# Attention in a four-layer kernel: block transposes of Q and K without duplicated columns, centred weights, norms from sums of squares, other virtual times, more PSUM banks

## The chip, the cores and the metric

One NeuronCore of a Trainium2 chip runs the whole program. The metric is the device time of one execution in microseconds (us); lower is better. The time before is 798.83 us, the median of three runs (794.63 to 799.25). A profile is one further execution: that of before took 792.66 us, of which the profile's span is 790.9 us.

Engines are named as in the profile: PE multiplies matrices, PEld loads its weights, DVE and ACT work on vectors, POOL is the small general engine, and SP issues DMAs. Each engine takes its instructions strictly in program order (weight loads may run ahead of multiplications). A multiplication of f32 data stands in the profile as two records.

## The reference

The input x has 16 sequences of 256 tokens with 256 channels. Four blocks follow, each inside a residual sum and a layer norm without weights:

```
x = _layernorm(x + _L0_attn_ref(x, ...))   # Fourier mixing, 16 heads
x = _layernorm(x + _L0_ffn_ref(x, ...))    # gated low-rank experts
x = _layernorm(x + _L1_attn_ref(x, ...))   # softmax attention
x = _layernorm(x + _L1_ffn_ref(x, ...))    # ternary weights, 1024 hidden
```

The first block multiplies x by two matrices, takes a Fourier transform over each head's 16 channels, normalises, takes a running sum of the second over the tokens, multiplies and transforms back. The second chooses one of eight experts per token by a gate (its score is divided by the squared distance of the token from an expert's centre) and adds the expert's rank-8 update; it scales x by one minus the gate. The third is attention with 16 heads of 16 channels:

```
qkv = jnp.einsum('bld,ed->ble', x, W_qkv)
qkv = qkv.reshape(b, 3, H, L, D_H)
Q, K, V = (qkv[:, 0], qkv[:, 1], qkv[:, 2])
scores = jnp.einsum('bhqd,bhkd->bhqk', Q, K) * D_H ** (-0.5)
attn = jax.nn.softmax(scores, axis=-1)
out = jnp.einsum('bhqk,bhkd->bhqd', attn, V)
out = out.transpose(0, 2, 1, 3).reshape(b, L, D_IN)
return jnp.einsum('bld,ed->ble', out, W_o)
```

The reshape is a plain one: the 256 x 768 numbers of one sequence, read in memory order, are cut into 48 pieces (16 heads each of Q, K, V) of 256 rows by 16. So token l gives the rows 48 l to 48 l + 47 of that list, and "row q of head h" is not token q.

The fourth block multiplies by ternary weights, squares a ReLU, normalises and multiplies back.

## The kernel before

**Stages.** The 16 sequences go in four groups of four (`GB`). Per sequence there is a front (`front`: blocks 1 and 2, up to the transposed result x2T) and a back (`back`: block 4); per group there is one `attention`. While the attention of group i runs, the fronts of group i + 1 and the backs of group i - 1 fill the gaps. Before the first attention stand loads, folded weights, the four fronts of group 0 and eight blocks of ternary weights; after the last stand four backs.

**Who sets the order.** All work is recorded as operations with a priority and an estimated cost on one or two engines. A list scheduler (`Order.run`) then walks through virtual time, gives each operation its engine and its buffer, and writes the instructions in that order. The order on each engine is therefore fixed before the program runs. An operation's priority (`order.prio`) is its virtual time: for group i, base = 100 (i + 1); projections of the attention (QKV) stand at base - 60, scores for the maximum at base + 6 (n - 8) for the n-th head, scores for the exponential and the product with V at base + 6 n, fronts of the next group at base + 23 + 20 g, backs of the group before at base + 20 + 20 g. `order.limit` bounds how many of the eight PSUM banks fronts and backs ("r", 4) and attention ("a", 6) may hold.

**Attention.** QKV is computed 32 tokens of all four sequences at a time (a token block, `tb`, L831): 512 and 256 columns. For the six token blocks that hold Q and K, DVE turns 32 x 32 blocks from PSUM into the tile `zt` (L840), in which sequence g owns partitions 32 g to 32 g + 31 and the 16 channels of a head lie on the first 16 of them. A head's piece is 16 columns wide, but a block is 32: so each 16-column piece is read twice (`to_broadcast([P, nj, 2, HD])`), and the second copy is not used. `zt` needs a 17th row per head: ones for K (`rowk`, L858) and minus the row maximum for Q (`rowq`, L914), both put there by DMAs of one partition each. V goes to DRAM (`vd`, L849) and comes back with its rows on partitions (`v`, L868).

For each head PE computes scores (L894, four sequences side by side, 16 rows each), DVE takes the negated maximum (`nm`, L903, four per head). After four heads the maxima are transposed (L907), copied (L908, `nmT`) and sent to the 17th row (8 DMAs if the heads' numbers are not consecutive, else 4). Then PE computes the scores again with 17 rows and the other way round (L933), ACT takes the exponential (L942), and PE multiplies by V (L948). The result is turned (L956), divided (L957, L960), transposed (L977), multiplied by `wo1` (L991) and added to x2 (L999).

**Norms.** `layernorm` takes mean and variance with two `bn_stats` (L569) and two `bn_aggr` (L571) on DVE, the power -1/2 on POOL (L563, L564), two more POOL steps for the bias (L573, L574), and the scaling of each half on DVE (L577) or ACT (L582), whichever the scheduler picks. It stands four times per sequence: after blocks 1, 2, 3 and 4. In a front ACT also squares x1 with a running sum (L723) for the distance in the gate.

**SP.** One queue issues all DMAs of the program. Its order, too, is the scheduler's, which counts 0.43 us per issue (`ISSUE`) and at least 1.6 us more to the landing.

Of the kernel before, what the change touches and what calls it, by code (L numbers as in the profile page):

```python
# [14 lines left out]
ALU = mybir.AluOpType  # L15
# [270 lines left out]
def forward(ctx, tc, x, xt, wq, wkv, wo0T, f0, degen, cs, wqkvT, wo1T, wfc, wproj, cst, out):  # L286
# [23 lines left out]
    ztv = zt_.rearrange("p (l j) -> p j l", j=NJ)  # L310
# [29 lines left out]
    order.limit = {("ps", "r"): 4, ("ps", "a"): 6, ("lane", "r"): 4}  # L340
# [155 lines left out]

    def ternary(n, w_dram, store):
# [68 lines left out]
    def layernorm(y, dst, extra=()):  # L566
# [8 lines left out]
        for t in range(2):  # L575
# [10 lines left out]
            op([(DVE, 0.36, on_dve), (ACT, 0.36, on_act)], [(dst, t)], [y, mv, rs, nb, *extra])  # L586
# [3 lines left out]
    def front(b, early):  # L590
# [123 lines left out]
        layernorm(y, x1, extra)  # L714
# [4 lines left out]
        x1sq, sq1 = stat(2), w(P, 2, D)  # L719
        for t in range(2):  # L720
            act(
                [(x1sq, t), (sq1, t)], [x1, *extra], 256 + 220,
                lambda t=t: A.activation(sq1.v[:, t, :], x1.v[:, t, :], AF.Square, accum_out=x1sq.v[:, t : t + 1]),  # L723
            )
# [80 lines left out]
        layernorm(y2, x2, extra)  # L805
# [13 lines left out]
    def attention(i):  # L819
# [4 lines left out]
        for n, tb in enumerate((5, 2, 0, 3, 6, 7, 1, 4)):  # L824
            order.prio = base - 60.0 + n
            for j0, nj in ((0, 32), (32, 16)):
# [10 lines left out]
                if tb < ZT:  # L837
                    dve(
                        [(z[tb], j0)], [b], nj * 32,
                        lambda b=b, tb=tb, j0=j0, nj=nj: V.transpose(  # L840
                            ztv[:, j0 : j0 + nj, ts(tb, 32)], b.v.unsqueeze(2).to_broadcast([P, nj, 2, HD])
                        ),
                        us=nj * 32 * 1.72e-3,
                    )
                if tb >= VT // 32:
# [7 lines left out]
                    )  # L853

            heads = [h for h in range(H) if k_at(h) == tb]
            for g in range(GB if heads else 0):
                op(
                    (SP, 0.1, lambda g=g, lo=ZQ + heads[0] * S, n=len(heads) * 2: nc.sync.dma_start(  # L858
                        zt_[32 * g + HD : 32 * g + HD + 1, lo : lo + n * P].rearrange("o (c q) -> o c q", q=P),
                        a(ones)[0:1, :].unsqueeze(1).to_broadcast([1, n, P]),  # L860
                    )),
                    [(rowk[tb], g)], [ones, z[tb]],
                )
        order.prio = base - 20.0
        for half, lo, n, at in ((0, 28, 4, 12), (0, 0, 12, 0), (1, 12, 16, 0)):
            for g in range(GB):
                op(
                    (SP, 0.5, lambda g=g, half=half, lo=lo, n=n, at=at: nc.sync.dma_start(  # L868
                        va[half][:, at : at + n, g, 0:HD],
                        vd.slot.ap[g].rearrange("t e -> (t e)")[(2 * ZQ + lo * P) * HD - VT * NJ * HD :][: n * P * HD].rearrange("(n p d) -> p n d", p=P, d=HD),  # L870
                    )),
                    [(v[half], (g, at))], [vd],
                )

        def part(g, rows, which, h, at=0, n=S):
            lo = which * ZQ + h * S + at
            return zt_[32 * g : 32 * g + rows, lo : lo + n]
# [7 lines left out]
        for q in range(4):  # L885
            nm, nmT, heads = tile_("nm", [P, GB, 4, 2]), tile_("nmT", [32, P]), HEADS[4 * q : 4 * q + 4]
            for k, h in enumerate(heads):
                order.prio = base + 6.0 * (4 * q + k - 8)
                sc = [ps([P, 2, S], "a") for _ in range(GB)]

                def go(sc=sc, h=h):
                    for t in range(2):
                        for g in range(GB):
                            T.matmul(  # L894
                                sc[g].v[:, t, :], part(g, HD, 0, h, t * P, P), part(g, HD, 1, h),
# [4 lines left out]
                for g in range(GB):  # L900
                    dve(
                        [(nm, (k, g))], [sc[g]], 512,
                        lambda nm=nm, sc=sc, g=g, k=k: V.tensor_reduce(nm.v[:, g, k, :], sc[g].v, AX.X, ALU.max, negate=True),  # L903
# [3 lines left out]
            pe([b], [nm, small], 0.11, lambda b=b, nm=nm: T.transpose(b.v, nm.v.rearrange("p g h t -> p (g h t)"), ident))  # L907
            act([nmT], [b], 128, lambda b=b, nmT=nmT: A.copy(nmT.v, b.v))  # L908
            runs = [heads] if heads[3] - heads[0] == 3 else [heads[0:2], heads[2:4]]
            for g in range(GB):  # L910
                for r, run in enumerate(runs):
                    n = len(run) * 2
                    op(
# [240 lines left out]
```

## Time and profile before

| what | value | where it is from |
|---|---|---|
| median of three runs | 798.83 us (794.63 to 799.25) | times |
| profiled execution, its span | 792.66 us, 790.9 us | times, page |
| granted TensorE clock, mean | 0.921 | times |
| instructions | 15,263 | page |
| QKV begins (L831), groups 0 to 3 | 100.1, 238.4, 421.5, 589.9 us | trace |
| first scores for the exponential (L933), groups 0 to 3 | 152.6, 291.4, 477.2, 642.4 us | trace |
| end of the last group's output projection (L991) | about 723 us | trace |

Busy time is the union of an engine's instructions. A PE that is "busy" may be at half clock, or a record may be stretched by a wait, so busy time is not work. In the view of windows each row gives a stretch, its length, and the busy time of each engine with the number of instructions, then the granted clock, the DMA share and GB/s. In the rows of instruction groups stand the line, engine, operation, tiles, shapes and number, then busy us, mean ns of one, and the idle time of the engine before them.

### The profile page before, as it was taken

To read this page: it belongs to the slowest core of one execution; us is meant where nothing else is said; L and a number is where in the kernel's file an instruction comes from. 1 tells how busy PE (TensorE), PEld (TensorE's weight loads), DVE (VectorE), ACT (ScalarE), POOL (GpSimd) and SP (SyncE) were. 2 spreads that over 40 slices of the span, in tenths; PEclk is the share of its full clock that TensorE was granted. 3 is DMA by queue.
4 is the path that set the end of the run, shared out by engine and by line. 5 is a ranking of instruction groups with operands and counts; after the bars stand their busy time and mean duration, and the time that the engine had idled before them with its cause. 6 is when DMAs were issued, how large, how long until landed. Compare 5 with 4: busy or idle time off the path is not lost.

```text
span 790.9 us, 15263 instructions
## 1 busy us (share of the span) xinstructions
PE 744.1 (94%) x5664; PEld 527.2 (67%) x5664; DVE 642.3 (81%) x1513; ACT 476.6 (60%) x942; POOL 124.0 (16%) x306
## 2 busy tenths in 40 slices
PE   9999499999999999999999999999989999999794
PEld 6786256665566667777676767765566787766784
DVE  1999989888987997998789999897567978756554
ACT  5865531238782238988765644966721297875973
POOL 1022000101110020222122012021020002011123
PEclk9999699679999988999999989997989699999986
DMA  8101015200001450001011350000001700000000
GB/s 292 40 27 41 13 24 79 57 15 16 29 15 25 67 69 2 16 27 30 2 40 49 60 38 16 15 16 2 15 1 35 76 10 16 14 16 15 1 28 27
DMA packets 87662, 27.18 MB, mean 34 GB/s; under 512 B 68700, under 2 KB 84900, under 8 KB 87588
## 3 DMA queue, kind: packets, MB, share of 16 engines
q1 hardware_dynamic: 87588, 26.21, 15.7%
q8 instruction: 45, 0.74, 0.4%
q14 instruction: 29, 0.24, 0.1%
HBM read 16.76 MB, written 8.91 MB: 32 GB/s over the span
## 4 chain that ended last, share of the span: by engine, by line
PE 68%; DVE 18%; ACT 9%; issue 3%; POOL 2%; DVEq 0%; ACTq 0%; POOLq 0%
PE bank L831 10%; PE bank L894 9%; PE bank L948 8%; PE bank L933 8%; PE bank L1056 7%; PE bank L609 5%; DVE nm L903 5%; PE bank L1027 5%; PE bank L991 3%; PE bank L708 3%; PE bank L793 2%; PE bank L732 2%; DVE st L569 2%; ACT zt L942 1%; ACT hi L1044 1%
## 5 line engine op out<-in xcount | busy, mean ns | idle before, releaser
L942 ACT ACTIVATE zt<-bank 128x512 f32<-128x512 f32 x256 | 133.4, 596 | 57.2 <-PE bank L933 52.3
L903 DVE TENSOR_REDUCE nm<-bank 128x2 f32<-128x512 f32 x256 | 158.8, 679 | 11.1 <-PE bank L894 10.2
L563 POOL TENSOR_SCALAR st<-st 128x2 f32<-128x2 f32 x80 | 23.4, 293 | 535.6 <-DVE st L571 369.7
L894 PE MATMUL bank<-zt 16*128 16x256 f32 x1024 | 100.4, 445 | 2.2 <-DVE nm L903 1.7
L894 PEld LDWEIGHTS bank<-zt 16*128 16x128 f32 x1024 | 63.7, 205 | 29.9 <-DVE nm L903 8.7
L831 PE MATMUL bank<-wqr,x2T 128*128 128x512 f32 (+1 forms) x256 | 83.2, 486 | 0.0
L933 PE MATMUL bank<-zt 17*128 17x256 f32 x1024 | 82.5, 415 | 0.3 <-DVE nm L903 0.3
L948 PE MATMUL bank<-zt,v 128*32 128x256 f32 x1024 | 78.6, 412 | 0.0
L1027 PE MATMUL bank<-xs,w1T 128*128 128x256 f32 x512 | 75.3, 299 | 0.5 <-DVE xs L1017 0.4
L1056 PE MATMUL bank<-w2T,hi 128*128 128x256 f32 x256 | 72.1, 312 | 3.5 <-ACT hi L1044 2.5
L1056 PE MATMUL bank<-w2T,lo 128*128 128x256 f32 x256 | 69.1, 302 | 6.0 <-DVE lo L1046 6.0
L1027 PEld LDWEIGHTS bank<-xs,w1T 128*128 128x128 f32 x512 | 67.6, 199 | 9.2 <-issue 3.7
L840 DVE STREAM_TRANSPOSE zt<-bank 128x1024 f32<-128x1024 f32 (+1 forms) x48 | 64.2, 1456 | 11.3 <-PE bank L831 5.0
L831 PEld LDWEIGHTS bank<-wqr,x2T 128*128 128x128 f32 x256 | 48.5, 190 | 34.2 <-issue 28.5
L933 PEld LDWEIGHTS bank<-zt 17*128 17x128 f32 x1024 | 51.8, 191 | 22.5 <-issue 12.4
L609 PE MATMUL bank<-wf,x 128*128 128x512 f32 x128 | 62.8, 623 | 0.0
L1056 PEld LDWEIGHTS bank<-w2T,hi 128*128 128x128 f32 x256 | 52.8, 206 | 14.1 <-issue 9.1
L564 POOL TENSOR_TENSOR st<-st,mhalf 128x2 f32<-128x2 f32 x80 | 59.4, 743 | 6.8 <-POOL st L563 0.2
L1056 PEld LDWEIGHTS bank<-w2T,lo 128*128 128x128 f32 x256 | 52.7, 206 | 7.5 <-DVE lo L1046 7.5
L1046 DVE TENSOR_TENSOR lo<-work,hi 128x512 fp32r<-128x512 f32 x64 | 42.7, 681 | 15.9 <-ACT hi L1044 15.8
L948 PEld LDWEIGHTS bank<-zt,v 128*32 128x32 f32 x1024 | 29.7, 114 | 35.1 <-issue 14.8
L1036 ACT ACTIVATE work<-bank 128x512 f32<-128x512 f32 x64 | 37.8, 591 | 20.4 <-PE bank L1027 16.2
(196 smaller groups left out, 1260.2 us busy)
## 6 DMA issues: line engine op xcount, KB each, us to landing
x<-in_xT SPq DMA_DIRECT2D x16, 256.0 KB
out<-work SPq DMA_DIRECT2D x16, 256.0 KB
x<-in_x SPq DMA_DIRECT2D x12, 256.0 KB
vd<-work SPq DMA_DIRECT2D x12, 256.0 KB
v<-vd SPq DMA_DIRECT2D x16, 128.0 KB
vd<-work SPq DMA_DIRECT2D x12, 128.0 KB
v<-vd SPq DMA_DIRECT2D x16, 96.0 KB
oT<-in_wfc SPq DMA_DIRECT2D x4, 256.0 KB
```

The costliest lines, as they stand in the source:

```text
L564: pool([dst], [dst, mhalf], 0.7, lambda: G.tensor_tensor(dst.v, dst.v, a(mhalf)[:, 0:n], ALU.pow))
L609: T.matmul(pb.v.rearrange("p a s k -> p (a s k)"), xT.v[:, c, ts(t, P)], a(wf)[:, c].rearrange("p a s f -> p (a s f)"), start=(c == 0), st ...
L831: T.matmul(b.v.rearrange("p j d -> p (j d)"), x2T.v[:, c, tb].rearrange("p g k -> p (g k)"), a(wqr)[:, c, j0 * HD : (j0 + nj) * HD], start ...
L840: lambda b=b, tb=tb, j0=j0, nj=nj: V.transpose(ztv[:, j0 : j0 + nj, ts(tb, 32)], b.v.unsqueeze(2).to_broadcast([P, nj, 2, HD])),
L894: T.matmul(sc[g].v[:, t, :], part(g, HD, 0, h, t * P, P), part(g, HD, 1, h), start=True, stop=True,)
L903: lambda nm=nm, sc=sc, g=g, k=k: V.tensor_reduce(nm.v[:, g, k, :], sc[g].v, AX.X, ALU.max, negate=True),
L933: T.matmul(sc[g].v[:, c, :], part(g, HD + 1, 1, h, c * P, P), part(g, HD + 1, 0, h), start=True, stop=True,)
L942: act([e], [sc[g]], 512, lambda e=e, sc=sc, g=g: A.activation(e.v, sc[g].v, AF.Exp, scale=HD ** -0.5))
L948: T.matmul(av.v[32 * g : 32 * g + 32, hk, :], v_part(g, h, c), es[g].v[:, c, :], start=(c == 0), stop=(c == 1),)
L1027: T.matmul(pb.v[:, i, :], a(w1T)[:, n // 2, ts(q * 2 + i, P)], xs.v[:, n % 2, n // 2, :], start=(n == 0), stop=(n == 3),)
L1046: dve([(lo, q)], [h, (hi, q)], 512, lambda h=h, part=part: V.tensor_tensor(part(lo), h.v, part(hi).bitcast(F32), ALU.subtract), us=0.63)
L1056: T.matmul(pw.v[:, t, :], part.v[:, k, ts(t, P)], a(w2T)[:, k, :], start=(k + n == 0), stop=(k + n == HID // P),)
```

## The change

Five things change together.

1. **Transposes without duplicates.** A block of 32 columns now holds two neighbouring heads' pieces, so one pass over 512 (or 256) columns turns all. The even pieces land on partitions 0 to 15 of each sequence's 32, the odd ones on 16 to 31. Four DMAs per token block (48 KB each, one per sequence) move the odd ones to partitions 0 to 15 of the second half of the 48 x 192 columns. Each head's rows now lie in two halves (even and odd), so the ones, the maxima and V's rows are written by twice as many DMAs, each half as long; the matrix products read the moving operand in two pieces of 128 columns.
2. **Centred weights.** `dg` (experts) and `wo1` get their mean over the output channels subtracted once, at the start. The sums before the second and third norm then have mean zero, because x1 and x2 have it already.
3. **Norms from sums of squares.** For those two norms ACT squares with a running sum instead of `bn_stats` and `bn_aggr` on DVE; the two POOL steps for the bias fall away. The squared length of x1 comes from its variance on POOL (three steps) instead of two squarings on ACT.
4. **Virtual times.** QKV moves from base - 60 to base, maxima from base - 48 + 6 n to base - 30 + 6 n, exponentials from base + 6 n to base + 10 + 6 n, fronts from base + 23 + 20 g to base + 20 g, backs from base + 20 + 20 g to base + 45 + 10 g. The estimate for scaling on ACT in `layernorm` goes from 0.36 to 0.53 us.
5. **PSUM banks.** The limits go from 4 to 5 (fronts and backs) and from 6 to 7 (attention).

```diff
+    ODD = ZT * 32 * NJ // 2
+    ztv = zt_[:, 0:ODD].rearrange("p (l j) -> p j l", j=NJ // 2)
+    zt2 = zt_[:, 0 : 2 * ODD].rearrange("p (t c) -> p t c", t=2)
...
-    order.limit = {("ps", "r"): 4, ("ps", "a"): 6, ("lane", "r"): 4}
+    order.limit = {("ps", "r"): 5, ("ps", "a"): 7, ("lane", "r"): 4}
...
+    def centred():
+
+        for t, at, n in ((dg, lambda: a(dg), 72), (wo1, lambda: a(wo1)[:, 0], P), (wo1, lambda: a(wo1)[:, 1], P)):
+            junk, m = tile_("work", [P, D]), stat(1)
+            act(
+                [junk, m], [t], 476,
+                lambda at=at, n=n, junk=junk, m=m: A.activation(
+                    junk.v[0:n, :], at(), AF.Identity, scale=-1.0 / D, accum_out=m.v[0:n, :]
+                ),
+            )
+            act(
+                [t], [t, m], 256,
+                lambda at=at, n=n, m=m: A.activation(at(), at(), AF.Identity, bias=m.v[0:n, :]),
...
+    def layernorm_of_centred(y, dst, extra=()):
+
+        vs, rs = stat(2), stat(2)
+        for t in range(2):
+            act(
+                [(vs, t), (dst, t)], [y, *extra], 256 + 220,
...
+                lambda t=t: A.activation(dst.v[:, t, :], y.v[:, t, :], AF.Square, accum_out=vs.v[:, t : t + 1]),
+            )
+        rsqrt(rs, lambda: vs.v, vs, 1.0 / D, LN_EPS, 2)
...
+            op([(DVE, 0.36, on_dve), (ACT, 0.36, on_act)], [(dst, t)], [y, rs, *extra])
...
+        mv, rs = layernorm(y, x1, extra)
...
-        x1sq, sq1 = stat(2), w(P, 2, D)
-        for t in range(2):
-            act(
-                [(x1sq, t), (sq1, t)], [x1, *extra], 256 + 220,
-                lambda t=t: A.activation(sq1.v[:, t, :], x1.v[:, t, :], AF.Square, accum_out=x1sq.v[:, t : t + 1]),
-            )
+
+        x1sq = stat(2)
+        pool([x1sq], [mv], 0.27, lambda: G.tensor_scalar(x1sq.v, mv.v[:, :, 1], float(D), None, ALU.mult))
+        for _ in range(2):
+            pool([x1sq], [x1sq, rs], 0.25, lambda: G.tensor_tensor(x1sq.v, x1sq.v, rs.v, ALU.mult))
...
-        layernorm(y2, x2, extra)
+        layernorm_of_centred(y2, x2, extra)
...
-            order.prio = base - 60.0 + n
+            order.prio = base + 0.0 + n
...
-                            ztv[:, j0 : j0 + nj, ts(tb, 32)], b.v.unsqueeze(2).to_broadcast([P, nj, 2, HD])
+                            ztv[:, j0 // 2 : (j0 + nj) // 2, ts(tb, 32)],
+                            b.v.rearrange("p (j t) d -> p j (t d)", t=2),
                         ),
-                        us=nj * 32 * 1.72e-3,
+                        us=nj * HD * 1.43e-3,
...
+            if tb < ZT:
+                width = 32 * NJ // 2
+                for g in range(GB):
+                    op(
+                        (SP, 0.1, lambda g=g, lo=tb * width: nc.sync.dma_start(
+                            zt_[32 * g : 32 * g + HD, ODD + lo : ODD + lo + width],
+                            zt_[32 * g + HD : 32 * g + 2 * HD, lo : lo + width],
+                        )),
+                        [(z[tb], ("odd", g))], [(z[tb], 0), (z[tb], 32)],
+                    )
...
-                order.prio = base + 6.0 * (4 * q + k - 8)
+                order.prio = base + -30.0 + 6.0 * (4 * q + k)
...
-                                sc[g].v[:, t, :], part(g, HD, 0, h, t * P, P), part(g, HD, 1, h),
+                                sc[g].v[:, t, :].rearrange("p (t q) -> p t q", t=2), some(g, HD, 0, h, t), every(g, HD, 1, h),
...
-                order.prio = base + 6.0 * n
+                order.prio = base + 10.0 + 6.0 * n
...
-            layernorm(y, x3)
+            layernorm_of_centred(y, x3)
...
-            base = 100.0 * (i + 1) + 20.0 + 20.0 * g
+            base = 100.0 * (i + 1)
             if i > 0:
-                order.prio = base
+                order.prio = base + 45.0 + 10.0 * g
                 back((i - 1) * GB + g, False)
             if i + 1 < NG:
-                order.prio = base + 3.0
+                order.prio = base + 0.0 + 20.0 * g
```

In the built order of the changed kernel SP issues 600 DMAs instead of 296 (192 for maxima instead of 96, 128 rows of ones instead of 64, 96 V loads instead of 48, and 96 moves of odd pieces). DVE scales 72 halves of norms instead of 50, and ACT 56 instead of 78.

## The prediction

> **What bounds the kernel now.** First the busy line and the slices: which engine could be the limit, and where.
>
> ```profile
> PE 744.1 (94%) x5664; PEld 527.2 (67%) x5664; DVE 642.3 (81%) x1513; ACT 476.6 (60%) x942; POOL 124.0 (16%) x306
> DVE  1999989888987997998789999897567978756554
> PEclk9999699679999988999999989997989699999986
> ```
>
> PE seems full, but it is busy also at half clock and while stretched by waits. So I counted PE's real work: every record by the shortest steady start-to-start time of its form in this trace (429 ns for 512 columns, 216 for 256, 109 for 128, 117 for the reduced-precision 256 columns of the back, 72 for the side-by-side ones, 16 of which take 1.15 us in the chain). The sum is 656.6 us. The span is 790.9 us, so 134 us are not filled: 21 before 100 us, 29 in the tail after 722 us, and 84 in the four groups. Windows show what stands in those places.
>
> ```profile
> 100.00:153.00 53.00, 52.57 (x285) 35.60 (x283) 47.32 (x76) 12.84 (x26) 1.71 (x5) 0.87 0.34 54
> 238.00:291.00 53.00, 53.00 (x313) 33.28 (x311) 47.52 (x84) 12.24 (x27) 3.33 (x11) 1.00 0.38 60
> 421.00:477.00 56.00, 54.76 (x346) 37.52 (x344) 52.33 (x92) 31.68 (x61) 5.98 (x11) 0.94 0.37 50
> 540.00:590.00 50.00, 44.68 (x374) 29.03 (x371) 29.02 (x91) 26.72 (x57) 8.13 (x24) 0.80 0.02 7
> 590.00:642.00 52.00, 51.64 (x289) 36.06 (x288) 44.28 (x65) 16.74 (x33) 3.75 (x11) 0.84 0.35 45
> 722.00:791.00 69.00, 51.63 (x327) 47.29 (x325) 38.71 (x92) 44.02 (x79) 18.34 (x40) 0.84 0.05 16
> ```
>
> Third number: PE, fifth: DVE, sixth: ACT. The first three and the fifth row are the openings of the groups, from QKV to the first exponential scores: 52 to 56 us each, with DVE 85 to 93% busy and ACT idle. Transposes (16.0 us per group by the same view for line L840) and maxima (19.8 to 22.3 us) are most of it. PE's counted work there is 43.4, 50.0, 48.0 and 40.6 us. The fourth row is the end of group 2, where no engine is full: QKV of group 3 waits for the last fronts. PE's work is 35.4 us of 50.
>
> Last, SP, since the first scores with 17 rows need its DMAs.
>
> ```profile
> SPq L868 <- DMA vd<-work: 33.7, 4, 8.4
> 144.71 5.03 SPq L914 DMA_DIRECT2D zt<-nmT  x8
> ```
>
> Each group waits about 8 us for V to land in DRAM before it is read back. Eight small issues take 5.03 us, 0.62 us each in steady pitch. In group 0 they end at 149.7 and L933 starts at 152.6, released by DVE: SP is just in time. In group 1 they end at 288.1 and L933 starts at 291.4, so 3.3 us to landing and start.
>
> **Transposes.**
>
> ```profile
> L840 DVE STREAM_TRANSPOSE zt<-bank 128x1024 f32<-128x1024 f32 x24 | 45.3, 1890 | 9.9 <-PE bank L831 5.0 <-DMA zt<-ones 2.9 <-ACT work L369 2.0
> L840 DVE STREAM_TRANSPOSE zt<-bank 128x512 f32<-128x512 f32 x24 | 24.5, 1022 | 1.4 <-ACT work L369 1.4
> L956 DVE STREAM_TRANSPOSE work<-bank 128x512 f32<-128x512 f32 x32 | 22.8, 712 | 24.6 <-PE bank L948 24.4
> L569 DVE BATCH_NORM_STATS2 st<-work 128x6 f32<-128x256 f32 x116 | 43.8, 415 | 0.7
> L571 DVE BATCH_NORM_AGGREGATE st<-st 128x2 f32<-128x6 f32 x128 | 18.6, 171 | 0.0
> L723 ACT ACTIVATE work<-work 128x256 f32<-128x256 f32 x28 | 11.4, 411 | 0.8 <-DMA vd<-work 0.8
> L723 ACT ACTIVATION_READ_ACCUMULATOR work<-work 128x1 f32 x28 | 5.5, 195 | 0.0
> L582 ACT ACTIVATE x<-work,st,st 128x256 f32<-128x256 f32 x35 | 20.0, 597 | 33.0 <-POOL st L574 32.8
> ```
>
> After there are 24 of 512 and 24 of 256 columns. By L956 (1.39 ns a column) that is 25.6 us, by the short L840 (2.00) 36.8. L956 writes contiguously, L840 with a stride as the new one does: I take 31. From 69.8 us this saves 39 (33 to 44) of DVE, some 8 us of each opening (busy union).
>
> **Norms.** 64 bn_stats and 64 bn_aggr go: 64 x 0.586 = 37.5 us of DVE. ACT gains 64 squares at 0.411 + 0.195 = 38.8 and loses 32, 19.4. The scheduler moves scalings: 22 more on DVE at 0.405 (L577), +8.9; ACT 59 fewer at 0.597 and 37 new ones with a scale alone, between 0.411 and 0.597, say 0.5: -16.7. Eight more evacuations on DVE at 0.686, +5.5, and 8 fewer on ACT, -4.7. Two squares of the back go to ACT, 1.3 each way. Centring is 6 ACT steps once, 3.3 us, in the first 50 us beside half-idle ACT; uncovered it costs 3.3. Sums: DVE -39 - 37.5 + 8.9 + 5.5 - 1.3 = -63, ACT about +3, POOL -17.1 + about 13. POOL's three steps for x1 lie beside the transposes and products of x1; if not, 0.8 us per front, 16 fronts. Strided `oT` copies and moving operands in two pieces I cost at nothing: two of 128 columns (218 ns) equal one of 256 (216). Bounds: if stride doubled a copy, 0.59 x 16 = 9 us on ACT, mostly covered.
>
> **SP.** 304 more issues at 0.62 are 188 us of SP. From the first V write to the end of the first maxima, group 0 has 44 issues before and 87 after. After: 87 x 0.62 = 54 us, plus three waits of about 2 us, each for a landed move before the ones may be written (bounds 0 and 3.3), plus 7 for V, plus 3.3 to the start: some 70 us from QKV's start instead of 52.5. With QKV at 96, L933 starts at 166, not 152.6. In groups 1 to 3 the new order lets QKV start beside the last heads of the group before and puts maxima ahead of V: 60, 47 and 47 issues to their end, 45 us with waits in group 1, against 47 us of PE work that stands before L933 there. But then L948 (product with V) waits for V: writes, 8 us, eight loads, landing. Counting what stands between, PE stalls in groups 1 to 3 about 16, 18 and 10 us, and behind a stalled L948 wait all later scores and the backs.
>
> The Trainium skill, page "DMA: Bandwidth & Descriptors", section "Rules for kernel authors", speaks against this part: transfers under 64 KB pay mostly overhead and should be made into one. With that page's fixed cost of about 2 us for each, strictly one after another, an estimate would be 608 us more. The trace overlaps them: 0.62 us of issue each.
>
> **The sum**, on the span of 790.9. Before group 0, DVE is 94% busy (74.85 of the 80 us from 20 on) and loses four norms of 1.17 us: -4. Group 0: L933 13 later, then 85 us with 74.5 of DVE shrink by 8: +5. Groups 1 to 3, opening to middle: counted gaps of 48 us before (3.0 + 10.5, 8.0 + 6.6, 11.4 + 8.5) against 44 of SP stalls: -4. End of group 2: fronts have earlier virtual times, QKV fills 10 of the 14.6 idle us: -10. Tail: one norm shorter, -1. Together -14: span 777, run 778.7 with the 1.8 around it. The run before (792.66) lies 0.8% under its median, so 785. PSUM limits and virtual times have no price of their own; they are in the order I counted.
>
> **Rivals.** *SP decides (slower).* If landings take 2 us more at the three or four waits of a group (4 x 4 x 2 = 32 us), or PE falls to half clock after each stall (before: 13.65 us long at 137 and 290 us, 7 lost each, 28 in all), some 30 come on top: 809, by the median 815. It decides once the first maxima land later than about 50 us after QKV starts; in group 0 they do. Against it: groups 1 to 3 start QKV earlier. *DVE's relief reaches PE (faster).* If SP keeps ahead, each opening shrinks by 6 us, 24 in all, with -4, -12 and -1: 752, by the median 758. For it: DVE is 85 to 93% busy in openings. Against: SP's count. *Nothing moves.* PE's order keeps as many gaps as before; DVE merely idles: 797.
>
> The Trainium skill, "TensorE: Matmul & The Clock Gate", Part 1, says an idle window of about 3.4 us halves the clock; rows here agree (0.80 in the idle end of group 2). It adds only to the first rival.
>
> **How the numbers follow.** Forecast 785 (own range 774 to 797): 45%. SP decides, 800 to 830: 25%. DVE's relief, 748 to 770: 18%. Nothing moves: 12%. The range 758 to 818 leaves out half of each outer case. Within 1% (791 to 807) a measurement of this kernel tells nothing from no change. Faster by more: 34 of the forecast's 45, the 18 and 2 of the last: 54. Slower: the 25, and 2 of each of the two middle cases: 29. Same: 17.
>
> **What would show it.** Right: DVE near 580 us; L840 near 31 us in all; L933 of group 0 at about 166 us with a gap released by the maxima's DMA; L831 no longer one block of 20.6 us; end of group 2 filled. Wrong: SP idle long before L933 (then the gain is larger), or L948 waiting over 20 us for V in several groups and a clock below 0.9 (then slower).

## The result and the profile after

The changed kernel takes 840.1 us (median of four runs, 838.45 to 842.61) against 798.81 us for the kernel before in the same comparison: ratio 1.0532, 95% interval 1.0486 to 1.0577. It is slower. Medians are of all runs, while ratios compare only runs in the faster of two states in which a kernel is found from one execution to the next, so a ratio need not be that of the medians. The profiled execution took 842.61 us, with a span of 840.8 us and a mean granted clock of 0.902 (before 0.921).

The page of the changed kernel: the busy line, and the slices of DVE and of the granted clock.

```profile
PE 762.3 (91%) x5664; PEld 531.1 (63%) x5664; DVE 609.2 (72%) x1413; ACT 477.3 (57%) x987; POOL 120.4 (14%) x290
DVE  2999869659977873979879584999567557952564
PEclk9999689779999995989999896999899688997986
```

DVE did lose work, 33 us of it, and PE is "busy" for 18 us longer with the same 5664 matrix instructions. By the shortest steady times the matrix work is the same in both kernels (654.6 us counted again for both), so the part of the span that PE does not fill went from some 136 to some 186 us. The clock row has fewer nines, 25 instead of 29: added up from the trace's record of the clock, PE stood at half clock for 168 us instead of 127.

The view of waits of the changed kernel, PE's rows that name a DMA (total us, number of times, longest us). Before, no row of PE in this view named a DMA.

```profile
PE bank L949 <- DMA zt<-zt: 22.9, 5, 7.8
PE bank L988 <- DMA zt<-nmT: 12.0, 6, 6.4
PE bank L1003 <- DMA v<-vd: 1.2, 3, 0.4
```

L949 are the scores for the maxima (L894 before) and wait for the moves of the odd pieces. L988 are the scores with 17 rows (L933 before) and wait for the maxima. L1003 is the product with V (L948 before); it hardly waits, so the stall that the prediction looked for there stands elsewhere. Where, the windows show: an opening and the stretch behind it for groups 0 and 1, then the end of group 2 and the stretch behind the opening of group 3, with the columns explained above.

```profile
98.00:153.00 55.00, 50.47 (x269) 31.59 (x267) 44.14 (x89) 13.18 (x29) 3.15 (x10) 0.93 0.26 50
153.00:174.00 21.00, 10.88 (x61) 5.25 (x53) 7.36 (x18) 4.41 (x10) 2.69 (x7) 0.58 0.41 47
245.00:298.00 53.00, 51.36 (x364) 30.70 (x357) 42.41 (x82) 19.93 (x51) 3.92 (x9) 0.97 0.16 32
298.00:342.00 44.00, 34.98 (x263) 24.42 (x267) 24.62 (x61) 18.29 (x37) 5.57 (x15) 0.81 0.39 55
580.00:620.00 40.00, 37.73 (x337) 22.37 (x338) 23.90 (x59) 21.24 (x49) 7.63 (x16) 0.87 0.09 22
652.00:700.00 48.00, 40.10 (x291) 32.22 (x293) 26.76 (x51) 27.52 (x50) 2.18 (x4) 0.72 0.38 48
```

The openings (first and third row) are nearly full. Behind the openings no engine is full: in the second row PE is busy for half of the time, at a clock of 0.58, and DVE for a third; in the fourth and sixth row the clock is 0.81 and 0.72. These two stretches and that in the second row follow the first maxima of their groups. What stands there in group 0 is in SP's timeline (start, us, instruction, number)

```profile
144.22 13.77 SPq L918 DMA_DIRECT2D v<-vd  x24
158.08 9.71 SPq L969 DMA_DIRECT2D zt<-nmT  x16
167.89 5.96 SPq L896 DMA_DIRECT2D zt<-zt  x8
```

and in PE's (the brackets: idle us before, and what ended it).

```profile
160.95 1.19 PE L988 MATMUL bank<-zt 17*128 17x256 f32 x2 [6.43 <-DMA zt<-nmT]
162.91 1.19 PE L988 MATMUL bank<-zt 17*128 17x256 f32 x2 [0.77 <-DMA zt<-nmT]
165.32 1.19 PE L988 MATMUL bank<-zt 17*128 17x256 f32 x2 [1.23 <-DMA zt<-nmT]
167.74 2.04 PE L988 MATMUL bank<-zt 17*128 17x256 f32 x10 [1.23 <-DMA zt<-nmT]
```

The maxima themselves had been ready for 20 us, as ACT's timeline shows.

```profile
138.10 0.24 ACT L963 COPY nmT<-bank 32x128 f32<-32x128 f32 x1
```

SP issues 24 loads of V before the first maxima, then 16 small DMAs of maxima at 0.61 us each. PE takes one sequence of a head after another as they land, two records of a head's 16 at a time. The whole head is done at 169.8; before, the first scores with 17 rows began at 152.6. In group 1 it is a move that PE waits for. SP's timeline first, then PE's:

```profile
303.30 15.35 SPq L918 DMA_DIRECT2D v<-vd  x24
318.75 2.78 SPq L896 DMA_DIRECT2D zt<-zt  x4
```

```profile
321.83 3.41 PE L949 MATMUL bank<-zt 16*128 16x256 f32 x16 [7.84 <-DMA zt<-zt]
```

DVE had turned token block 4 by 298.6 us, but its four moves stand behind 24 loads of V on SP, and PE stands for 7.8 us. The same gap is in groups 2 and 3, with 5.0 and 6.2 us; there 4 and 5 DMAs of ones stand between the loads and the moves as well. In the trace's record of the clock, half clock begins 1.9 to 2.9 us after PE stops in each of these four long stands (6.43, 7.84, 4.99 and 6.17 us) and lasts for 13.7 to 20.5 us. By group, the time that PE does not fill is:

| us not filled by PE | before | after | difference |
|---|---|---|---|
| up to group 0 | 23.2 | 21.8 | -1.4 |
| group 0 | 21.7 | 33.4 | +11.7 |
| group 1 | 13.2 | 28.9 | +15.7 |
| group 2 | 29.3 | 35.6 | +6.3 |
| group 3 | 20.0 | 37.7 | +17.7 |
| tail | 28.8 | 28.9 | +0.1 |

The tail is counted from the start of the last group's last output projections (722.5 us before); they end at 729.7, not at about 723.

Last, the groups of instructions after, where the change saved work: the two shapes of the transposes, and the new squares on ACT.

```profile
L877 DVE STREAM_TRANSPOSE zt<-bank 128x512 f32<-128x512 f32 x24 | 34.8, 1449 | 17.6 <-PE bank L867 16.9 <-issue 0.4 <-PE bank L1003 0.4
L877 DVE STREAM_TRANSPOSE zt<-bank 128x256 f32<-128x256 f32 x24 | 19.8, 823 | 4.7 <-PE bank L867 4.3 <-ACT work L372 0.4
L613 ACT ACTIVATE x<-work 128x256 f32<-128x256 f32 x60 | 24.5, 413 | 30.5 <-DVE work L1054 24.4 <-DVE work L836 5.9
```

The transposes cost 54.6 us, not 31: half the columns, but 2.83 and 3.2 ns a column where there were 1.85 and 2.00.

### The profile page after: what moved, and what is told of

It reads as the page before. It is cut to its first block, busy times and chain, and to the rows that moved or that the text cites. A ratio compares the mean times of both kernels' runs of the same rounds, so it can differ in the third digit from the quotient of the medians.

```text
span 840.8 us, 15583 instructions
## 1 busy us (share of the span) xinstructions
PE 762.3 (91%) x5664; PEld 531.1 (63%) x5664; DVE 609.2 (72%) x1413; ACT 477.3 (57%) x987; POOL 120.4 (14%) x290
## 4 chain that ended last, share of the span: by engine, by line
PE 63%; DVE 13%; SPq 8%; DMA 6%; ACT 5%; issue 3%; POOL 1%; DVEq 0%; ACTq 0%; POOLq 0%
PE bank L949 9%; PE bank L1003 8%; PE bank L988 8%; PE bank L1111 7%; PE bank L867 6%; PE bank L1082 6%; SPq L918 5%; PE bank L646 4%; DMA vd<-work 4%; PE bank L1046 3%; DVE zt L877 2%; PE bank L745 2%; PE bank L573 2%; SPq L969 2%; PE bank L768 1%
## 5 line engine op out<-in xcount | busy, mean ns | idle before, releaser
L949 PE MATMUL bank<-zt 16*128 16x256 f32 x1024 | 98.0, 436 | 23.0 <-DMA zt<-zt 22.9
L988 PE MATMUL bank<-zt 17*128 17x256 f32 x1024 | 93.0, 436 | 13.6 <-DMA zt<-nmT 12.0
L949 PEld LDWEIGHTS bank<-zt 16*128 16x128 f32 x1024 | 61.1, 200 | 56.2 <-issue 23.7
L867 PE MATMUL bank<-wqr,x2T 128*128 128x512 f32 (+1 forms) x256 | 94.8, 514 | 1.6 <-DVE zt L877 1.4
L988 PEld LDWEIGHTS bank<-zt 17*128 17x128 f32 x1024 | 56.9, 200 | 44.0 <-issue 20.5
L1003 PE MATMUL bank<-zt,v 128*32 128x256 f32 x1024 | 80.6, 423 | 1.5 <-DMA v<-vd 1.2
L1111 PE MATMUL bank<-w2T,lo 128*128 128x256 f32 x256 | 72.0, 309 | 7.4 <-DVE lo L1101 7.4
L1111 PE MATMUL bank<-w2T,hi 128*128 128x256 f32 x256 | 75.0, 320 | 3.5 <-ACT hi L1099 2.8
L1082 PEld LDWEIGHTS bank<-xs,w1T 128*128 128x128 f32 x512 | 70.5, 210 | 7.8 <-issue 3.5
L877 DVE STREAM_TRANSPOSE zt<-bank 128x512 f32<-128x512 f32 (+1 forms) x48 | 52.4, 1136 | 22.3 <-PE bank L867 21.2
L1091 ACT ACTIVATE work<-bank 128x512 f32<-128x512 f32 x64 | 37.7, 589 | 33.9 <-PE bank L1082 33.8
L1003 PEld LDWEIGHTS bank<-zt,v 128*32 128x32 f32 x1024 | 29.7, 116 | 42.8 <-issue 19.9
L1101 DVE TENSOR_TENSOR lo<-work,hi 128x512 fp32r<-128x512 f32 x64 | 42.4, 681 | 11.5 <-ACT hi L1099 11.4
```

The costliest lines, as they stand in the source:

```text
L867: T.matmul(b.v.rearrange("p j d -> p (j d)"), x2T.v[:, c, tb].rearrange("p g k -> p (g k)"), a(wqr)[:, c, j0 * HD : (j0 + nj) * HD], start ...
L877: lambda b=b, tb=tb, j0=j0, nj=nj: V.transpose(ztv[:, j0 // 2 : (j0 + nj) // 2, ts(tb, 32)], b.v.rearrange("p (j t) d -> p j (t d)", t=2),),
L949: T.matmul(sc[g].v[:, t, :].rearrange("p (t q) -> p t q", t=2), some(g, HD, 0, h, t), every(g, HD, 1, h), start=True, stop=True,)
L988: T.matmul(sc[g].v[:, c, :].rearrange("p (t q) -> p t q", t=2), some(g, HD + 1, 1, h, c), every(g, HD + 1, 0, h), start=True, stop=True,)
L1003: T.matmul(av.v[32 * g : 32 * g + 32, hk, :], v_part(g, h, c), es[g].v[:, c, :], start=(c == 0), stop=(c == 1),)
L1082: T.matmul(pb.v[:, i, :], a(w1T)[:, n // 2, ts(q * 2 + i, P)], xs.v[:, n % 2, n // 2, :], start=(n == 0), stop=(n == 3),)
```

## The experiments

The theory: SP's added DMAs (600 where there were 296) meet an order on PE that the scheduler drew up with too cheap a price for them, 0.43 us an issue and 1.6 us to the landing, against some 0.62 and 3 in the trace. PE stands in that order behind scores whose maxima or moves have not landed, and runs at half clock after each long stand. The rivals: the new virtual times alone make the loss; the new instructions (dearer transposes, work moved to ACT) make it; or landing, not issuing, does.

### The parts alone

**The traffic alone.** The kernel before, with every added DMA of the change but none of its other parts: ones, maxima and V in two halves each, and 96 moves of 48 KB that copy the unused duplicates over the pieces that they equal.

```diff
+            if tb < ZT:
+                for g in range(GB):
+                    op((SP, 0.1, lambda ...: nc.sync.dma_start(
+                        zt_[32 * g : 32 * g + HD, lo : lo + width],
+                        zt_[32 * g + HD : 32 * g + 2 * HD, lo : lo + width])),
...
+                for t in range(2):
```

> The kernel before, with the SP traffic of the changed one and nothing else of it: rows of ones, maxima and V in twice as many DMAs of half the length, and 96 moves of 48 KB whose data are already in place. Theory 1 (SP's queue is the loss): its first exponential scores come 10 to 20 us later in each group, and the time rises by 25 to 45 us, to 825 to 845 us. Theory 2 (the new virtual times, that is the order of PE's work, are the loss): the order here is nearly that of before, so 795 to 808 us.

865.65 us, ratio 1.0839 (1.078 to 1.0899). DVE keeps the work of before (644.1 us), yet the time grows by more than with the whole change. The view of waits of this kernel has one PE row with a DMA:

```profile
PE bank L947 <- DMA zt<-nmT: 24.0, 10, 8.5
```

L947 are the scores with 17 rows here; they begin at 161.9 in group 0 instead of 152.6. The traffic, in an order drawn up at the old figures, is enough to make the loss.

**The traffic on another queue.** The changed kernel, with moves and ones issued by ACT. The scheduler counts 0.62 us on ACT for each of them and 2.0 us more to the landing, and for SP the figures of before.

```diff
-                        (SP, 0.1, lambda g=g, lo=tb * width: nc.sync.dma_start(
+                        (ACT, 0.62, lambda g=g, lo=tb * width: nc.scalar.dma_start(
...
-                        (SP, 0.1, lambda g=g, t=t, ...: nc.sync.dma_start(
+                        (ACT, 0.62, lambda g=g, t=t, ...: nc.scalar.dma_start(
```

> The changed kernel, with the 96 moves and the 128 rows of ones issued from ACT's queue instead of SP's; SP then issues 376 instead of 600. Theory 1 (SP's queue): the first exponential scores of group 0 come at 140 to 150 us instead of 161, and the time falls from 840 to 790 to 815 us. Theory 2 (virtual times): 830 to 845 us, since the order of PE's work stays.

874.02 us, ratio 1.0964 (1.0904 to 1.1023). It does not decide: the first scores with 17 rows begin at 172.7 us in group 0, later than in the changed kernel, and ACT's own work now waits for DMAs. My reading, not tested, is that it stands behind DMAs that wait for their data. ACT's worst rows with a DMA in the view of waits:

```profile
ACT work L689 <- DMA zt<-nmT: 27.1, 1, 27.1
ACT xs L1073 <- DMA v<-vd: 26.2, 2, 20.7
```

**The norms alone.** The kernel before with the centred weights, `layernorm_of_centred`, the squared length of x1 on POOL, and the estimate of 0.53 for ACT's scaling.

```diff
-        layernorm(y2, x2, extra)
+        layernorm_of_centred(y2, x2, extra)
```

> The kernel before, with centred weights and norms from sums of squares alone; old transposes, times and limits. Theory 1 (SP's queue; DVE's relief is real where SP does not hide it): 780 to 793 us, DVE some 24 us less busy. Theory 2 (the order decides, and what an engine has to do hardly matters): 795 to 810 us.

795.56 us, ratio 0.9979 (0.9944 to 1.0014). DVE falls from 642.3 to 616.3 us and the time does not move: this relief is worth nothing by itself. None of it falls in the openings: from QKV to the first scores with 17 rows DVE is busy for 194.9 us in the four groups together, and for 191.3 before. So the run says nothing of what a relief in the openings would bring.

**The virtual times alone.**

```diff
-            order.prio = base - 60.0 + n
+            order.prio = base + 0.0 + n
...
-                order.prio = base + 6.0 * (4 * q + k - 8)
+                order.prio = base + -30.0 + 6.0 * (4 * q + k)
```

with those of exponentials, fronts and backs as in the change.

> The kernel before with the new virtual times alone (QKV, scores, fronts, backs); its transposes, norms, limits and its 296 DMAs stay. Theory 1 (SP's traffic is the loss): 785 to 805 us, since QKV fills the end of group 2 and nothing is added to SP. Theory 2 (the new order is the loss): 815 to 840 us.

822.72 us, ratio 1.0306 (1.0227 to 1.0385), with 15.4 us of PE waiting for maxima in three places. So the new times alone lose too, though SP has only the DMAs of before. That speaks for the first rival, unless here too the order is only drawn up with too cheap a price; the same times with the two numbers, below, decide.

**The transposes alone,** with their moves and halved DMAs, at the old times and old norms.

```diff
-                            ztv[:, j0 : j0 + nj, ts(tb, 32)], b.v.unsqueeze(2).to_broadcast([P, nj, 2, HD])
+                            ztv[:, j0 // 2 : (j0 + nj) // 2, ts(tb, 32)],
+                            b.v.rearrange("p (j t) d -> p j (t d)", t=2),
```

> The kernel before with the new transposes alone, which bring the moves of odd pieces and the DMAs of half the length; old times, norms and limits. Theory 1 (SP's traffic): 845 to 865 us, as the run with SP's traffic alone (865), less at most 15 us of transposes saved. Theory 2 (the order): 785 to 805 us.

863.05 us, ratio 1.0797 (1.0714 to 1.088); PE waits 20.4 us for maxima, in eleven places. The cheaper transposes do not make up for the DMAs that they need.

**A transpose by itself.** The kernel before, with 32 more transposes of 128 x 512 after its end, whose result is not used: contiguous, and with steps of 24, 25, 32 and 48 elements between the numbers of a row in the result; at 24 and 48 also with the duplicated reading, at 24 also from SBUF.

```diff
+        V.transpose(zt_[:, 0:512], bank[:, 0:512])
+        V.transpose(wide(24), bank[:, 0:512].rearrange("p (j d) -> p j d", d=32))
...
+        V.transpose(wide(48), bank[:, 0:256]....to_broadcast([P, 16, 2, HD]))
```

> The kernel before, with 32 transposes of 512 columns behind its end, to measure one by itself: contiguous result, results with a step of 24, 25, 32 and 48 elements, the step of 48 and of 24 with each 16 columns read twice, and the step of 24 from SBUF. If the step of the result sets the price: 0.71 us contiguous, 1.45 us at 24, about 1.0 at 48 whatever is read. If reading twice made the old one cheap: 1.45 at all steps read once, 1.0 where read twice. The time is not compared; it grows by some 35 us.

One execution, 828.12 us with the added work. From the groups of the stretch at its end (step 24, 48, 48 read twice, 32, contiguous):

```profile
L1116 DVE STREAM_TRANSPOSE zt<-bank 128x512 f32<-128x512 f32 x4 | 5.8, 1446 | 0.1
L1119 DVE STREAM_TRANSPOSE zt<-bank 128x512 f32<-128x512 f32 x4 | 4.1, 1029 | 0.1
L1120 DVE STREAM_TRANSPOSE zt<-bank 128x512 f32<-128x512 f32 x4 | 4.2, 1052 | 0.1
L1118 DVE STREAM_TRANSPOSE zt<-bank 128x512 f32<-128x512 f32 x4 | 4.2, 1047 | 0.1
L1115 DVE STREAM_TRANSPOSE zt<-bank 128x512 f32<-128x512 f32 x3 | 2.1, 717 | 0.1
```

Reading each number twice costs little: 1052 against 1029 ns at step 48, 1444 against 1446 at step 24. The step of the result sets the price: the change halved the columns and with them the step, from 48 to 24, and the same 512 columns then take 1.4 times as long. Step 25 took 1137 ns, and step 24 from SBUF 1452.

### The scheduler's price of a DMA

**The change with figures near the measured ones.** The work stays, but for its order and for which engine takes a step that either may take.

```diff
-ISSUE = 0.43
+ISSUE = 0.62
...
-                o.end = moved = max(at + ISSUE + 1.6, moved + cost)
+                o.end = moved = max(at + ISSUE + 2.7, moved + cost)
```

> The changed kernel, but its scheduler counts 0.62 us for an issue on SP instead of 0.43 and 2.7 us to the landing instead of 1.6, as measured; it may therefore place other work ahead of what waits for DMAs. Theory 1 (SP's traffic, and an order made for a faster SP): 800 to 828 us. Theory 2 (virtual times): 832 to 848 us.

795.9 us, ratio 0.9953 (0.9906 to 1.0). The two numbers bring 44 of 840 us back. PE's rows with these DMAs in the view of waits:

```profile
PE bank L949 <- DMA zt<-zt: 3.0, 2, 2.2
PE bank L988 <- DMA zt<-nmT: 2.1, 2, 1.8
```

5.1 us instead of 34.9. PE's unfilled time is again near that of before (some 139 us), and half clock falls from 168 to 99 us. Group 0 shows how. SP's timeline and PE's first scores with 17 rows, then the window of the long stand above:

```profile
154.17 9.72 SPq L969 DMA_DIRECT2D zt<-nmT  x16
161.30 0.79 PE L988 MATMUL bank<-zt 17*128 17x256 f32 x6
153.00:174.00 21.00, 16.88 (x102) 12.15 (x102) 13.93 (x48) 9.25 (x18) 5.87 (x16) 0.65 0.22 32
```

The 16 maxima still stand behind 24 loads of V, begin 3.9 us sooner and take the same 9.7 us, and the scores begin no sooner (161.30 against 160.95 us). But PE is busy for 16.88 of the 21 us instead of 10.88, because work of the fronts now stands ahead of these scores and between them. The DMAs are all still there: SP was not too slow for this work, only for this order.

**The same two numbers in the kernel before.**

> The kernel before, its scheduler counting 0.62 us per issue on SP and 2.7 us to the landing. Theory 1 (an order made for a faster SP is the loss, in proportion to the DMAs): with 296 DMAs little is wrong in it, 785 to 803 us. Theory 3 (the better numbers help any order, and the gain they brought to the changed kernel, 44 us, says nothing of its DMAs): 750 to 775 us.

796.37 us, ratio 1.0002 (0.9974 to 1.003). With 296 issues and the old virtual times the wrong price showed no cost.

**The virtual times alone, with the two numbers.**

> The kernel before with the new virtual times alone, its scheduler counting 0.62 and 2.7 us. Theory 1: the 24 us that the new times cost came from maxima that start later and meet SP behind time, so it falls from 823 to 785 to 805 us. Theory 2 (the new times are worse by themselves): 812 to 830 us.

786.56 us, ratio 0.9865 (0.9814 to 0.9916). The new times gain 1.35% if the order counts DMAs near their price and lose 3.1% if it does not, so the first rival falls.

**The transposes alone, with the two numbers** and the new PSUM limits.

> The kernel before with the new transposes, moves and DMAs and the new PSUM limits (old times, old norms), its scheduler counting 0.62 and 2.7 us. Without the better numbers and the limits it took 863 us. Theory 1: most of the 64 us come back, 800 to 825 us; what stays is SP's 190 us of issues themselves. Theory 2 (SP's traffic costs whatever the order): 845 to 865 us.

807.33 us, ratio 1.0133 (1.0081 to 1.0185), with 1.3 us of PE waiting for a DMA. 56 us better than without (the limits had no part that shows in the pair with and without them, below), yet still slower than before: the transposes of this change, at a fitting order too, showed no gain.

**One number at a time, in the changed kernel.** First the issue alone, at 0.61,

> The changed kernel, its scheduler counting 0.61 us per issue on SP, and 1.6 us to the landing as before. If the queue of issues is what the order had wrong (some 60 to 90 issues ahead of the first exponential scores, 0.18 us short on each, 11 to 16 us): 795 to 812 us, nearly all of the way back from 840. If the landing is: 825 to 842 us.

820.75 us, ratio 1.026 (1.0183 to 1.0337); then the landing alone at 2.7.

> The changed kernel, its scheduler counting 2.7 us to the landing, and 0.43 us per issue as before. If the queue of issues is what the order had wrong: 822 to 842 us. If the landing (1.1 us short at each of the chained waits): 795 to 812 us.

854.53 us, ratio 1.0699 (1.0639 to 1.0758). The issue alone brings 19 of the 44 us; the landing alone brings none (it was 14 us slower than the change). Of these orders only that with both gave 796.

**Dearer still,** 0.64 and 3.0.

> The changed kernel, its scheduler counting 0.64 us per issue and 3.0 us to the landing, a little more than measured. If the recovery to 796 us comes from counting SP enough, and not from one lucky order: 785 to 808 us again. If it was luck: anything up to 845, as with 1.6 or 0.43.

816.75 us, ratio 1.0248 (1.0169 to 1.0326), with no PE wait for maxima or moves at all. The expectation put 785 to 808 us if counting SP enough was what brought the change back, so the size of the recovery, 44 us, is in part that of one lucky order. Its direction holds: with this work, the two orders drawn with 0.43 us an issue take 840 and 855 us, the three with 0.61 to 0.64 take 796, 817 and 821, and a fourth, with 552 DMAs (below), 795. So the absence of these waits is not enough: orders drawn up with nearly the same figures lie 20 us apart. Which detail of the order makes these 20 us was not tracked down and stays open; a single pair of kernels with differences of this size shows less than its interval says.

### Fewer issues, and the better version

**Ones by one DMA per sequence,** in the kernel before: 248 DMAs instead of 296, at the old figures.

```diff
-            for g in range(GB if heads else 0):
...
+        for g in range(GB):
+            op((SP, 0.1, lambda g=g: nc.sync.dma_start(
+                zt_[32 * g + HD : 32 * g + HD + 1, ZQ : 2 * ZQ]....
```

> The kernel before, with the rows of ones of all 16 heads written by one DMA per sequence instead of four: 12 issues fewer per group ahead of the first maxima, 248 in all instead of 296. Theory 1 (SP's queue limits the openings): 780 to 794 us. Theory 2 (SP has slack in the kernel before; DVE and the order decide): 794 to 804 us.

795.7 us, ratio 0.9973 (0.9935 to 1.0011). Twelve issues fewer per group show no gain there.

**The change with the two numbers, prices for V's transfers,** and the ones of the odd halves written in group 0 alone, since nothing writes over them later (552 DMAs).

```diff
-                        (SP, 0.1, lambda st=st, tb=tb, j0=j0, nj=nj: nc.sync.dma_start(
+                        (SP, 1.2 * nj / 32, lambda st=st, tb=tb, j0=j0, nj=nj: nc.sync.dma_start(
...
-                for t in range(2):
+                for t in range(1 if i else 2):
```

> The changed kernel, its scheduler counting 0.62 and 2.7 us, also 1.2 us of transfer for each 256 KB of V written and 0.13 us for each 128 rows of V read; and the ones of the odd halves written in group 0 only (552 DMAs instead of 600), since nothing overwrites them. Theory 1: below the 796 us of the better numbers alone, 770 to 792 us. Theory 2 (what is left is not SP's): 790 to 805 us.

794.94 us, ratio 0.998 (0.9955 to 1.0006). No more than with the two numbers alone.

**Without the new transposes:** new times, new norms and the two numbers, on the transposes of before; with the new PSUM limits, and without.

```diff
-    order.limit = {("ps", "r"): 4, ("ps", "a"): 6, ("lane", "r"): 4}
+    order.limit = {("ps", "r"): 5, ("ps", "a"): 7, ("lane", "r"): 4}
```

> The kernel before with everything of the change but the transposes and their DMAs, that is new virtual times, centred weights and norms, and PSUM limits; its scheduler counts 0.62 and 2.7 us. Theory 1 (the transposes bring more DMA issues than they save DVE time; the rest helps once SP is counted rightly): 772 to 788 us, below the 787 of the times alone, and below both kernels. Theory 2 (DVE's relief by the transposes is needed too): 788 to 800 us.

784.76 us, ratio 0.9806 (0.9734 to 0.9879).

> The same without the new PSUM limits. If the limits help: 3 to 10 us above the run with them. If they do not: within 3 us of it or below; 772 to 792 us in all.

787.64 us, ratio 0.9792 (0.972 to 0.9865). The limits make no difference that shows, and the norms little: with the new times and the two numbers alone it was 0.9865, and the intervals overlap. The first of the two beats both kernels. The busy line and clock of its page:

```profile
PE 725.8 (93%) x5664; PEld 508.3 (65%) x5664; DVE 619.3 (79%) x1395; ACT 483.6 (62%) x1005; POOL 115.9 (15%) x290
PEclk9999699597999999999999999999899999999986
```

DVE does 10 us more than in the changed kernel, and the clock row is nearly all nines. It differs from the changed kernel with the two numbers (0.9953) in the transposes and their DMAs alone; with the pair above (807.33 against before) they cost 1.3 to 1.5% where the order suits them. Two pairs of one sign, with a scatter of orders as large as seen above, make this likely, not certain.

**The better version with one DMA of ones per sequence.**

> New times, norms and limits with the old transposes, counting 0.62 and 2.7 us, and the ones of all heads in one DMA per sequence (248 DMAs instead of 296). If SP still binds there: 770 to 782 us. If not: 782 to 792 us, as without.

792.66 us, ratio 0.995 (0.991 to 0.9991): slower than without the edit, though it has fewer DMAs. It waits for the last of the four token blocks of K before any ones are written, and in its view of waits PE waits for DMAs of ones for 3.7 us, which it does not in the better version. That is part of the 8 us between the two; whether the rest is more of this or the scatter of orders was not tested.

The half-clock time (of the profiled execution) rises with the run time (the median) over most of these kernels:

| kernel | time, us | at half clock, us |
|---|---|---|
| better version | 784.8 | 84 |
| times alone, two numbers | 786.6 | 91 |
| change, two numbers | 795.9 | 99 |
| transposes alone, two numbers | 807.3 | 130 |
| change, 0.64 and 3.0 | 816.8 | 143 |
| change, issue alone | 820.8 | 127 |
| virtual times alone | 822.7 | 139 |
| the change | 840.1 | 168 |
| change, landing alone | 854.5 | 192 |
| transposes alone | 863.1 | 190 |
| traffic alone | 865.7 | 213 |
| change, moves and ones on ACT | 874.0 | 208 |

I read it as a consequence of the stands: the two numbers change hardly any instruction, only the order, and in the changed kernel half clock begins within each of the four long stands. The issue alone stands off the line, and so do kernels with the DMAs and virtual times of before (before 127 us; norms alone 132 us at 795.6; before with the two numbers 142 us at 796.4). The Trainium skill, "TensorE: Matmul & The Clock Gate", Part 1, says that an idle window of about 3.4 us halves the clock. The rows agree with the direction, since the clock in the stretch of group 0 with the gap of 6.43 us is 0.58, though half clock began after 1.9 to 2.9 us; no run here moved the length of a gap by itself.

## Why the prediction was wrong

It forecast 785 and measured 840.1, outside the range of 758 to 818. The mechanism had stood there as the rival "SP decides", with 815 and 25%; it was too cheap by 25 us. Of the prediction's two signs for that case neither came: the product with V waited for 1.2 us, not 20, and the mean clock was 0.902, not below 0.9.

**The step that failed** is "Groups 1 to 3, opening to middle: counted gaps of 48 us before (3.0 + 10.5, 8.0 + 6.6, 11.4 + 8.5) against 44 of SP stalls: -4." It set the stalls in the place of the gaps. In the trace they came on top: without the end of group 2 (14.5 us before, 5.2 after) groups 1 to 3 have 48 us unfilled before and 97 after, +49 instead of -4. In these three groups PE waited for a DMA for 23.8 us, and its half clock grew from 61.5 to 102.4 us, worth at most half of the difference, 20.5: together at most 44 us, as much as the prediction had put for the stalls. What failed is the other term: the 48 us of gaps, which it counted as filled, did not go. Which of the old gaps stayed was not traced one by one. Over the whole run the waits are 36 us.

**What it overlooked in that step.** Only the waits for maxima and V were looked for behind the openings. The scores for the maxima wait too, for moves behind 24 loads of V (7.8, 5.0 and 6.2 us in groups 1 to 3), while V itself cost 1.2 us: the 44 us came out near, but from other waits and from the clock, and that is luck. The clock stood in the prediction only as a rival's price. And the sum took the order on PE as given, though the prediction itself used 0.62 us and 3.3 us where the scheduler counts 0.43 and 1.6. The question was not how many issues stand ahead but whether PE's order had been made for them; bringing the two figures near the trace brought 44 us back in one order; the issue alone, and both made dearer still, brought 19 and 23.

**Group 0,** "+5", measured +11.7, of which direct waits for a DMA are 12.4; half clock there is 27.3 us in both kernels. The first scores were put at 166 us; they began at 160.9 and ran without breaks from 167.7, released by the maxima's DMA. That part was right. "85 us with 74.5 of DVE shrink by 8" did not come: from these scores to the next QKV it was 84.4 us against 85.8 before. Behind the wait DVE is busy for 7.36 of 21 us, and with the norms alone this stretch did not shrink either (90.1 us).

**Transposes,** 31 us put, 54.6 measured; saved 15, not 39. The bounds (L956, contiguous, and L840, step 48) shared the belief that a column has a price whatever the step; step 24 lies outside both. DVE came to 609 us, not 580. DVE was not what PE waited for in the long stands, so I take this error to have cost little of the time here; no run shows it by itself.

**Norms.** The saving on DVE alone was 26 us against the -24 that follow from the working (-37.5, +8.9, +5.5, -1.3): right in size, worth nothing.

**Near:** the ends. "End of group 2: ... -10" measured -9 (14.5 to 5.2; the fifth row of the windows, which holds it, has PE busy for 37.73 of 40 us); "Before group 0 ... -4" measured only -1.4; "Tail ... -1" measured 0.

**The rival "DVE's relief reaches PE"** (758) falls with the result, and its condition, that SP keeps ahead, was not met. The norms alone do not test it, since their relief lies outside the openings; what a relief in the openings would bring without added DMAs stays open. "Nothing moves" falls with the result too. The rule of the Trainium skill, "DMA: Bandwidth & Descriptors", section "Rules for kernel authors", that transfers under 64 KB pay mostly overhead, spoke against the moves of 48 KB; the kernel with the traffic alone (+8.4%) agrees that these DMAs were dear here, but with an order drawn up for them the changed kernel, with all its small DMAs, stood at 0.9953, so that the rule does not settle their price.

**Open:** which gaps of before stayed in groups 1 to 3, what makes orders with nearly the same figures 20 us different, and whether these transposes would gain in the kernel with a step other than 24; none of these was tried.

## What to carry to other kernels

When a change adds many small DMAs to a queue, compare the planner's price of an issue and of a landing with the pitch in the trace before anything else: here two constants decided between 840 and 796 us, and orders with nearly the same constants still lay 20 us apart, so one pair of kernels proves little. Before a saving on an engine goes into a sum, see in which stretch it falls: the norms alone took 26 us off DVE, none of it in the openings, and the run became no shorter. Halving the numbers that an instruction handles need not halve its time if the step of its result changes with them.

## What was not expected of the hardware

The 32 x 32 transpose of 128 x 512 f32 on DVE took 717 ns into contiguous columns, 1446, 1137, 1047 and 1029 ns at steps of 24, 25, 32 and 48 elements: the smallest of the four steps is the dearest, and one element more makes it a fifth cheaper. The Trainium skill, "SBUF — State Buffer", section "Door 1: The DMA port swizzle", tells of lines of 16 bytes and of a penalty for each access that goes to a new one. That fits the step from 717 to over 1000 ns; all four larger steps go to a new line each time, so it does not tell why 24 costs 1.4 times what 48 does.
